# A graph layer's edge sums: a quarter of the late chunk products as two float32r parts, a larger share of the sort comparisons on VectorE, and the folding of weights in sixteen steps

## The chip, the cores and the metric

The kernel runs on one NeuronCore of a Trainium2 chip. The metric is the device time of one execution in microseconds (us). The engines are TensorE (PE, with its weight loads shown as PEld), VectorE (DVE), ScalarE (ACT), GpSimd (POOL) and SyncE (SP, which here only issues DMAs). Each engine runs its instructions in program order.

## What is computed

A message-passing layer of a graph network. 206,250 edges carry a row of 128 float32 values each; the rows are summed by the node named in `src`; the sums go through three dense layers together with the node rows `x` and a global row; the result is added to `x` and normalised.

```
edge_aggr = zeros((n, 128)).at[row].add(edge_features)        # n = 6250 nodes
combined  = concat([x, edge_aggr, global_expand], -1) @ W_c + b_c
h = softplus(combined @ W1 + b1)
h = softplus(h @ W2 + b2)
out = layernorm(x + (h @ W3 + b3))
```

## The kernel before

The nodes are cut into 32 buckets of 196 (`BL`). The edges lie in 1692 columns of 122 rows; two columns make a pair, so there are 846 pairs, in eight groups; three pairs make a piece (`PAIRS`), which gives 286 pieces. The work has three stages, most of it overlapped:

- **Sort and scatter.** For each group the positions of its edges are worked out (`positions`: counting matmuls in bf16 and small DVE steps, lines 498 to 764; line 498 compares `pair_block` with a table, both in SBUF). For each piece a one-hot matrix of 6 x 128 columns is made from the edges' slots (`compare`, lines 1137 to 1142): on DVE as one comparison with a table in PSUM, on ACT as six `Abs` activations and one `Relu`. Even pieces are DVE's, odd ones ACT's (`SHARE = 2`). `gather` (line 1153) sorts the rows by a matmul with this matrix, two units of three matmuls a piece; `settle` (line 1165) copies each unit from PSUM into one of six pair buffers (`SETS`), two ACT copies a unit; `scatter_row` (line 1182) writes one pair's rows to their places in `rows_by` in HBM by an indirect DMA that POOL issues: 846 of them. Places that may stay empty are filled beforehand (`fill_rows`, DMAs on SP from a constant tile of 7 rows a partition, `FILL`).
- **Sum.** `rows_by` comes back in chunks of 128 rows, each with rows of one bucket only (or of two neighbours). `load` brings up to eight chunks into one of six buffers (`AHEAD`), by SP; `match` (line 990) makes a one-hot matrix of 196 columns a chunk on DVE, with the table of nodes in PSUM; `product` (line 1013) multiplies, one float32 matmul a chunk, which the trace shows as two records (1758 products, 3516 records); `add` (line 1036) adds the finished PSUM sums into `sums_t`, on DVE. The unit of match and product is up to four chunks (`HALF`); there are 512 units.
- **Layers.** `node_layers` (lines 1356 to 1440) runs the dense layers tile by tile, with `Abs`, `Exp` and `Ln` on ACT and the maxima, sums and statistics on DVE. `fold` and the biases (`c_bias`, `z_bias`, `b2_c`, `b3_all`) are folded from the weights by `node_rows`, ahead of that.

The order is written out by a planner in the kernel. Every step gets a planned time: a scattered row every 1.3 us (`SCATTER`) from 24 us (`FIRST`), comparisons, gathers and evictions so many us ahead of their rows (`COMPARED`, `GATHERED`, `SETTLED`), the steps of an ACT comparison spread over 0.65 us each, from `SPREAD` earlier on; each load after its rows are scattered, each match two units ahead of its product (`TOGETHER`; four in the tail, `AT_END`), each product when the one before it is planned to be over. The steps sorted by time are the program of PE, DVE, ACT and SP. What is planned later than the last row (1123.8 us) is the rest, which `node_layers` takes up between its tiles, in the same order. The two steps of `node_rows` (lines 1070 to 1097) are planned in the second half of the fourth group.

Of the kernel before, what the change touches and what calls it, by code (L numbers as in the profile page):

```python
# [6 lines left out]

F32 = mybir.dt.float32
BF16 = mybir.dt.bfloat16
F16 = mybir.dt.float16  # L10
# [8 lines left out]
P = 128  # L19

BL = 196
# [29 lines left out]

FILL, DUE = 7, 8
ROW = 136
# [93 lines left out]
def kernel(  # L147
# [171 lines left out]
    with ExitStack() as phase:  # L319
        rows_p = phase.enter_context(tc.tile_pool(name="rows", bufs=ROWS))  # L320
        sort_p = phase.enter_context(tc.tile_pool(name="sort", bufs=3))
        pairs_in = phase.enter_context(tc.tile_pool(name="pairs_in", bufs=2))
# [28 lines left out]
        def scratch(name):  # L351
            return per.tile([P, 4 * P], F32, name=name, bufs=1)

# [52 lines left out]
        def fill_rows():  # L406
# [10 lines left out]
            def some(due, b, n, lo, rows, k):  # L417
                to = rows_by.rearrange("(s j) c -> s j c", j=STRIDE * P)[b:b + n, lo:lo + rows * k, :]
                ins = sync_dma(to.rearrange("b (p k) c -> p b (k c)", k=k),
                               fill[:rows, :k * ROW].unsqueeze(1).to_broadcast([rows, n, k * ROW]))  # L420
                apart(ins, "direct", ["scatter"])
                fills.setdefault(due, []).append(ins)

            def doubtful(b, mixed):
                if mixed:
                    start, end, twice, room, per = ROOM * P, STRIDE * P, 2, MIXED_ROOM / 2, MIXED_PER
                else:
                    start, end, twice, room, per = 0, rooms[b] * P, 1, rooms[b], ROWS_PER[kind[b]]
                lo = start + twice * int(certain(mixed, gap_at, room, per))
                hi = end - twice * untouched(mixed, per)  # L430
                rows, k = min(((rows, -(-(hi - lo) // rows)) for rows in (96, 112, P)),
                              key=lambda e: (e[0] * e[1], -e[0]))
                assert k <= FILL and lo + rows * k <= end
                return lo, rows, k
# [451 lines left out]
        def sum_steps():  # L886
# [36 lines left out]
            base_of = {v: min(bs) for v, bs in in_visit.items()}  # L923
            chunks, hots_of, parts_of, met, begun = {}, {}, {}, {}, set()
            awaits = [0]
# [52 lines left out]

            def match(n):
                j, a, e = units_of[n]  # L980
                hot = hots.tile([P, HALF, BL], F32, name="hot")
                hots_of[n] = hot
                q = a
                while q < e:
                    lo = hi = place_in(j, q)
                    step, m = 1, 1
                    while q + m < e and place_in(j, q + m) > hi and (m == 1 or place_in(j, q + m) == hi + step):
                        step, hi = place_in(j, q + m) - hi, place_in(j, q + m)
                        m += 1
                    nc.vector.tensor_tensor(  # L990
                        hot[:, q - a:q - a + m],
                        chunks[j][:, lo:hi + 1:step, D:W].to_broadcast([P, m, BL]),
                        iota_ps.unsqueeze(1).to_broadcast([P, m, BL]), op=ALU.is_equal)
                    q += m

            pending = []

            def product(n):
# [9 lines left out]
                for q in range(a, e):  # L1008
# [3 lines left out]
                    last = met[v].count(b) == in_visit[v].count(b)  # L1012
                    nc.tensor.matmul(part[:, b - base_of[v], :], t[:, place_in(j, q), :D], hot[:, q - a],  # L1013
                                     start=first, stop=last)
                if n == last_unit[j]:
# [24 lines left out]
            found, load_at, match_at, product_at, freed, at = [], {}, [], {}, {}, 0.0  # L1040
            opened = -1
            for n, (j, a, e) in enumerate(units_of):
# [23 lines left out]
        def node_rows():  # L1066

            steps = []

            def combine():  # L1070


                small = small_bank()
                nc.tensor.matmul(small[:, 0, :1], of_weights["wc2"], cols[:, 3:4],
                                 start=True, stop=True)
                nc.vector.tensor_add(c_bias, small[:, 0, :1], cols[:, 0:1])
                small = small_bank()
                for k in range(2):
                    nc.tensor.matmul(small[:, k, :], of_weights[f"wc{k}"], w_sb["w1"],
                                     start=True, stop=True)  # L1080
                nc.vector.tensor_copy(fold, small[:, :2, :])

            def biases():
                small = small_bank()
                nc.tensor.matmul(small[:, 0, :1], w_sb["w1"], c_bias, start=True, stop=True)
                nc.vector.tensor_add(z_bias, small[:, 0, :1], cols[:, 1:2])

                nc.vector.tensor_scalar(neg_z, z_bias, -1.0, None, op0=ALU.mult)
                small = small_bank()
                nc.tensor.matmul(small[:, 0, :1], w_sb["w2"], z_bias, start=True, stop=True)  # L1090
                nc.vector.tensor_add(b2_c, small[:, 0, :1], cols[:, 2:3])
                nc.vector.tensor_scalar(neg_b2, b2_c, -1.0, None, op0=ALU.mult)
                b2_all = per.tile([P, P], F32, name="b2_all", bufs=1)
                nc.vector.tensor_scalar(b2_all, ones, b2_c, None, op0=ALU.mult)
                small = small_bank()
                nc.tensor.matmul(small[:, 0, :], b2_all, w_sb["w3"], start=True, stop=True)
                nc.vector.tensor_add(b3_all, small[:, 0, :], of_weights["b3"])

            return [combine, biases]

# [30 lines left out]
        def compare(i):  # L1131
# [3 lines left out]
            hot = hot_of[i] = sort_p.tile([P, 2 * PAIRS, P], F32, name="sort_hot")  # L1135
            if i % SHARE == 0:
                return [lambda: nc.vector.tensor_tensor(  # L1137
# [56 lines left out]
        with tc.manual_schedule(engines={ET.PE, ET.DVE, ET.Activation, ET.SP}):  # L1194
# [71 lines left out]
            for i, t in enumerate(begins):  # L1266
                mine = units(i)
                soon = 0.0 if i else SOON
                if i % SHARE == 0:
                    when(t - COMPARED - soon, lambda i=i: compare_next(i))  # L1270
# [346 lines left out]
```

## Time and profile before

| | |
|---|---|
| median of 3 runs | 1289.03 us (1283.15 to 1290.0) |
| the profiled execution | 1289.92 us |
| its span in the trace | 1288.2 us |
| PE busy | 1167.7 us (91%) |
| DVE busy | 1027.6 us (80%) |
| ACT busy | 1003.9 us (78%) |
| POOL busy | 880.9 us (68%) |
| DMA, mean | 297 GB/s, 381.96 MB |

A row of waits reads: engine and line, what it waited for, us in total, times, longest. A row of groups reads: line, engine, operation, tiles, shapes, count, then the busy time in us and the mean ns of one, then the idle time ahead of them and what ended it. A row of the sums by stretch gives the stretch and its length, the busy time and count of each engine, the granted TensorE clock, the DMA engines' share and GB/s. A row of the timeline or of the chain of waits begins with start and duration in us.

### The profile page before, as it was taken

What the parts mean: (1) busy time and instruction counts of PE and PEld (TensorE: products, weight loads), DVE (VectorE), ACT (ScalarE), POOL (GpSimd) and SP (SyncE); (2) the same over time, 40 slices, a digit from 0 to 9 for tenths busy, and PEclk for the clock granted to TensorE, in tenths of its full rate; (3) what the DMA queues carried; (4) which work ended last, traced back from release to release, by engine and by line L of the source; (5) the groups of instructions that cost most, each with busy time, mean ns of one, the idle gap of its engine ahead of it and who ended that gap; (6) DMA issues with size and microseconds to landing.
All of it is one profiled execution on the core that took longest, in us unless ns stands there. A gap on an engine that the chain in (4) does not pass through costs nothing.

```text
span 1288.2 us, 26304 instructions
## 1 busy us (share of the span) xinstructions
PE 1167.7 (91%) x8617; PEld 1111.8 (86%) x8617; DVE 1027.6 (80%) x2260; ACT 1003.9 (78%) x2335; POOL 880.9 (68%) x915
## 2 busy tenths in 40 slices
PE   5778898888998998999899999999999999899893
PEld 5667788877988898989899999999999999898772
DVE  7868977888789977899878887789876767687784
ACT  5897987899687888977998888988899999403343
POOL 2777777777577776776777777777777777750334
PEclk9788998989999998999999999999999999999996
DMA  6789998899999997997999999999999999874421
GB/s 248 240 296 347 344 334 288 305 344 355 339 327 331 362 330 278 319 325 246 322 309 309 323 336 328 345 313 335 316 350 334 369 336 363 288 218 140 140 75 53
DMA packets 174636, 381.96 MB, mean 297 GB/s; under 512 B 27546, under 2 KB 118626, under 8 KB 160670
## 3 DMA queue, kind: packets, MB, share of 16 engines
q1 hardware_dynamic: 130751, 260.70, 61.2%
q0 software_dynamic: 41328, 115.65, 23.1%
q10 hardware_dynamic: 2415, 3.85, 0.9%
q8 instruction: 72, 1.18, 0.4%
q14 instruction: 70, 0.57, 0.1%
HBM read 242.47 MB, written 142.20 MB: 299 GB/s over the span
## 4 chain that ended last, share of the span: by engine, by line
PE 65%; DVE 12%; ACT 8%; DMA 7%; issue 4%; POOL 3%; SPq 0%; ACTq 0%; DVEq 0%; POOLq 0%
PE part L1013 37%; PE sorted L1153 21%; ACT pairs L1165 4%; DMA rows_by<-pairs,pair 4%; POOL rows_by L1182 3%; ACT sort_hot L1140 3%; DMA chunks<-rows_by 3%; DVE hot L990 2%; DVE past L727 1%; PE small L557 1%; PE small L559 1%; ACT sort_hot L1142 1%; DVE sort_hot L1137 1%; DVE sums_t L1036 1%; PE small L1395 1%
## 5 line engine op out<-in xcount | busy, mean ns | idle before, releaser
L1182 POOL DMA_INDIRECT rows_by<-pairs,pair x846 | 828.1, 979 | 298.3 <-issue 202.8
L1013 PE MATMUL part<-hot,chunks 128*128 128x196 f32 x3516 | 675.1, 335 | 13.2 <-DVE sums_t L1036 9.9
L1165 ACT COPY pairs<-sorted 64x387 f32<-64x387 f32 (+2 forms) x1144 | 542.6, 474 | 118.8 <-PE sorted L1153 95.7
L1013 PEld LDWEIGHTS part<-hot,chunks 128*128 128x128 f32 x3516 | 582.0, 193 | 21.9 <-DVE sums_t L1036 11.3
L1153 PE MATMUL sorted<-rows,sort_hot 122*128 122x129 f32 x3384 | 498.5, 288 | 44.5 <-ACT sort_hot L1142 32.0
L1153 PEld LDWEIGHTS sorted<-rows,sort_hot 122*128 122x128 f32 x3384 | 457.6, 199 | 53.5 <-ACT sort_hot L1142 36.3
L990 DVE TENSOR_TENSOR hot<-chunks,both_ps 128x784 f32<-128x784 f32 (+3 forms) x541 | 426.1, 809 | 9.2 <-DMA chunks<-rows_by 9.0
L1140 ACT ACTIVATE sort_hot<-plain,slot 122x128 f32<-122x128 f32 x840 | 292.8, 394 | 18.6 <-PE sorted L1153 6.3
L1036 DVE TENSOR_TENSOR sums_t<-sums_t,part 128x392 f32<-128x392 f32 (+1 forms) x262 | 143.5, 548 | 134.0 <-PE part L1013 133.0
L1137 DVE TENSOR_TENSOR sort_hot<-slot,both_ps 122x768 f32<-122x768 f32 x143 | 134.5, 940 | 1.9 <-PE sorted L1153 1.0
L1142 ACT ACTIVATE sort_hot<-sort_hot 122x768 f32<-122x768 f32 x143 | 118.6, 830 | 3.9
L1437 POOL TENSOR_SCALAR y<-y,mv,rs 128x128 f32<-128x128 f32 x40 | 31.1, 785 | 93.8 <-DVE rs L1425 93.5
L576 DVE TENSOR_REDUCE slot<-small 122x16 f32<-122x512 f32 (+2 forms) x109 | 72.9, 668 | 21.5 <-PE small L559 20.7
L1367 ACT ACTIVATE away<-sorted,z_bias 128x512 f32<-128x512 f32 (+2 forms) x13 | 8.5, 656 | 72.9 <-PE sorted L1357 72.9
L498 DVE TENSOR_TENSOR pair_ib<-pair_block,plain 122x512 bf16<-122x512 bf16 (+2 forms) x157 | 63.4, 411 | 0.2
L557 PE MATMUL small<-pair_ib,half 122*122 122x512 bf16 (+2 forms) x109 | 43.3, 398 | 7.6 <-DVE slot L576 7.5
L742 PEld LDWEIGHTS <-past 128*128 128x128 f16 x424 | 25.4, 100 | 17.9 <-DVE past L727 12.7
L727 DVE TENSOR_TENSOR past<-both_ps,starts 128x512 f16<-128x512 f32 (+1 forms) x61 | 39.8, 664 | 1.2 <-PE small L742 0.9
L742 PE MATMUL small<-jump,past 128*128 128x56 f16 (+3 forms) x424 | 29.4, 190 | 11.8 <-DVE past L727 8.4
L559 PEld LDWEIGHTS <-starts_h 128*122 128x122 bf16 x236 | 25.3, 148 | 11.9 <-issue 7.7
L1114 ACT COPY rows<-pair_i 122x16 f32<-122x16 f32 x106 | 22.2, 209 | 17.0 <-DMA rows<-in_edge 16.4
L727 DVE TENSOR_TENSOR past<-both_ps,starts_late 128x512 f16<-128x512 f32 (+2 forms) x49 | 32.3, 661 | 0.0
(163 smaller groups left out, 515.6 us busy)
## 6 DMA issues: line engine op xcount, KB each, us to landing
rows<-in_edge SPq DMA_DIRECT2D x105, 1032.0 KB
chunks<-rows_by SPq DMA_DIRECT2D x362, 136.0 KB
chunks<-rows_by SPq DMA_DIRECT2D x203, 204.0 KB
chunks<-rows_by SPq DMA_DIRECT2D x75, 272.0 KB
rows_by<-pairs,pair POOLq DMA_INDIRECT x846
rows_by<-fill SPq DMA_DIRECT2D x10, 1249.5 KB
rows_by<-fill SPq DMA_DIRECT2D x10, 714.0 KB
chunks<-rows_by SPq DMA_DIRECT2D x13, 408.0 KB
```

Source lines behind the costliest of these rows:

```text
L498: nc.vector.tensor_tensor(ib, cols.unsqueeze(2).to_broadcast([PN, m, SB, QUAD]), bucket_at[:PN].unsqueeze(1).to_broadcast([PN, m, SB, QUAD ...
L576: nc.vector.tensor_reduce(to, of, axis=mybir.AxisListType.X, op=ALU.max)
L727: nc.vector.tensor_tensor(past[:, :, a:b], twice_ps[:KB].unsqueeze(1).unsqueeze(1).to_broadcast([KB, 2, b - a, P // 2]), own["starts"][:, ...
L990: nc.vector.tensor_tensor(hot[:, q - a:q - a + m], chunks[j][:, lo:hi + 1:step, D:W].to_broadcast([P, m, BL]), iota_ps.unsqueeze(1).to_bro ...
L1013: nc.tensor.matmul(part[:, b - base_of[v], :], t[:, place_in(j, q), :D], hot[:, q - a], start=first, stop=last)
L1036: nc.vector.tensor_add(here, here, of)
L1137: return [lambda: nc.vector.tensor_tensor(hot[:PN, :2 * m], slot[:PN, at:at + 2 * m].unsqueeze(2).to_broadcast([PN, 2 * m, P]), slot_ps[:P ...
L1140: return [lambda j=j: nc.scalar.activation(hot[:PN, j], by_slot[:PN], AF.Abs, bias=slot[:PN, at + j:at + j + 1], scale=-1.0) for j in rang ...
L1142: for j in range(2 * m)] + [lambda: nc.scalar.activation(hot[:PN, :2 * m], hot[:PN, :2 * m], AF.Relu, bias=1.0, scale=-1.0)]
L1153: nc.tensor.matmul(out[:, j, :], hot[:PN, at], rows_at[col // LOAD_COLS][:PN, col % LOAD_COLS, :], start=True, stop=True)
L1165: nc.scalar.copy(sets_at[i][64 * n:64 * n + 64, lo:lo + m, h, :W], out[64 * h:64 * h + 64, :m, :])
L1182: s = nc.gpsimd.indirect_dma_start(out=dst, out_offset=bass.IndirectOffsetOnAxis(ap=at, axis=0), in_=rows[:, j].rearrange("p a b -> p (a b ...
```

## The change

Five things change together.

- **Fine units.** Of the units planned later than 650 us, every fourth (every third after the last row is planned) is multiplied in two float32r parts, if it has over two chunks that lie in one run; units planned from 30 us before to 12 us after the last row are left out. ACT copies the unit's rows to a float32r tile (`high`), DVE writes the rest, rows minus high, over the rows (`low`), and each chunk takes two float32r matmuls, high and rest, instead of one float32 matmul.
- **Sort comparisons.** Of five pieces two are ACT's (the second and the fourth) and three DVE's; ACT's steps are planned 4.5 us ahead instead of 2; there are four buffers for the one-hot matrices instead of three.
- **Folding.** `node_rows` is sixteen steps (three of them empty) instead of two, spread over the same time.
- **Fill.** The constant tile has 4 rows a partition instead of 7, and a fill of more is issued as two DMAs.
- **Buffers.** Five instead of six `hot` tiles, `scratch` tiles of half the width, two `high` tiles.

```diff
-FILL, DUE = 7, 8
+FILL, DUE = 4, 8
-SHARE, SPREAD = 2, 2.0
+BY_ACT, SHARE, SPREAD = (1, 3), 5, 4.5
+FINE_FROM, FINE_EVERY, HIGHS, COARSE = 650.0, (4, 3), 2, (-30.0, 12.0)
-    hots = ctx.enter_context(tc.tile_pool(name="hots", bufs=6))
+    hots = ctx.enter_context(tc.tile_pool(name="hots", bufs=5))
-        sort_p = phase.enter_context(tc.tile_pool(name="sort", bufs=3))
+        sort_p = phase.enter_context(tc.tile_pool(name="sort", bufs=4))
-                ins = sync_dma(to.rearrange("b (p k) c -> p b (k c)", k=k),
-                               fill[:rows, :k * ROW].unsqueeze(1).to_broadcast([rows, n, k * ROW]))
+                to = to.rearrange("b (p k) c -> p b (k c)", k=k)
+                for a in range(0, k, FILL):
+                    w = min(FILL, k - a) * ROW
+                    ins = sync_dma(to[:, :, a * ROW:a * ROW + w],
+                                   fill[:rows, :w].unsqueeze(1).to_broadcast([rows, n, w]))
...
+            def high(n):
+                high_of[n] = sums_p.tile([P, HALF, D], F32R, name="high", bufs=HIGHS)
+                for to, at, m in runs_of(n):
+                    nc.scalar.copy(high_of[n][:, to], chunks[units_of[n][0]][:, at, :D])
+
+            def low(n):
+                for to, at, m in runs_of(n):
+                    rows = chunks[units_of[n][0]][:, at, :D]
+                    nc.vector.tensor_tensor(rows.bitcast(F32R), rows, high_of[n][:, to].bitcast(F32),
+                                            op=ALU.subtract)
...
-                    nc.tensor.matmul(part[:, b - base_of[v], :], t[:, place_in(j, q), :D], hot[:, q - a],
-                                     start=first, stop=last)
+                    rows, by = t[:, place_in(j, q), :D], hot[:, q - a]
+                    if n in fine:
+                        nc.tensor.matmul(part[:, b - base_of[v], :], high_of[n][:, q - a], by,
+                                         start=first, stop=False)
+                        nc.tensor.matmul(part[:, b - base_of[v], :], rows.bitcast(F32R), by,
+                                         start=False, stop=last)
+                    else:
+                        nc.tensor.matmul(part[:, b - base_of[v], :], rows, by.bitcast(F32),
+                                         start=first, stop=last)
...
+                since += 1
+                if (product_at[n] > FINE_FROM and since >= FINE_EVERY[product_at[n] > ends[-1]]
+                        and not COARSE[0] < product_at[n] - ends[-1] < COARSE[1] and e - a > 2 and len(runs_of(n)) == 1):
+                    since = 0
+                    fine.add(n)
+                    found.append((max(match_at[n], product_at[n] - 4.0), len(found), lambda n=n: high(n)))
+                    found.append((max(match_at[n] + 1.0, product_at[n] - 1.5), len(found), lambda n=n: low(n)))
...
-            return [combine, biases]
+            return [
+                lambda: product_of("c", (of_weights["wc2"], cols[:, 3:4], 1)),
+                lambda: product_of("fold", *((of_weights[f"wc{k}"], w_sb["w1"], D) for k in range(2))),
+                lambda: v.tensor_add(c_bias, got("c"), cols[:, 0:1]),
+                lambda: v.tensor_copy(fold, banks_of["fold"][:, :2, :]),
+                lambda: product_of("z", (w_sb["w1"], c_bias, 1)),
+                lambda: None,
...
-            if i % SHARE == 0:
+            if i % SHARE not in BY_ACT:
```

More of the change, by code (lines that the diff above doesn't have):

```diff
@@ L1066, in node_rows @@
         def node_rows():
[L1068 to L1097, printed above, removed]
@@ L1099, in node_rows, with product_of, got, b2_rows @@
-            return [combine, biases]
+            banks_of, v = {}, nc.vector
+            def product_of(name, *pairs):
+                small = banks_of[name] = small_bank()
+                for k, (of, by, w) in enumerate(pairs):
+                    nc.tensor.matmul(small[:, k, :w], of, by, start=True, stop=True)
+            def got(name, k=0, w=1):
+                return banks_of[name][:, k, :w]
+            b2_all = []
+            def b2_rows():
+                b2_all.append(per.tile([P, P], F32, name="b2_all", bufs=1))
+                v.tensor_scalar(b2_all[0], ones, b2_c, None, op0=ALU.mult)
```

45 lines of the change are left out of this document (31 added, 14 removed).

## The prediction

> **What bounds the kernel now.** I read the 40 slices first, then the waits, then sums by stretch, the groups by shape, and the timeline where a price was missing.
>
> ```profile
> POOL 2777777777577776776777777777777777750334
> ```
> ```profile
> core 0: us, PE busy (x) PEld busy (x) DVE busy (x) ACT busy (x) POOL busy (x), PEclk, DMA share, GB/s
> 60.00:650.00 590.00, 523.17 (x4154) 500.38 (x4155) 491.31 (x1173) 499.10 (x1173) 434.81 (x444) 0.95 0.91 321
> 650.00:1110.00 460.00, 458.80 (x3393) 453.82 (x3392) 357.56 (x598) 410.82 (x965) 350.48 (x360) 1.00 0.96 330
> 1128.00:1157.00 29.00, 29.00 (x163) 28.79 (x164) 24.50 (x40) 0.00 (x0) 15.47 (x16) 0.94 0.73 211
> 1157.00:1260.00 103.00, 95.75 (x485) 76.98 (x484) 80.57 (x194) 42.62 (x71) 22.17 (x30) 1.00 0.39 117
> ```
>
> Three stages, each with its own limit. The scatter stage issues 846 rows on GpSimd (POOL). Its waits, first for 60 to 650 us, then for 650 to 1110 us:
>
> ```profile
> POOL rows_by L1182 <- issue: 108.9, 355, 0.6
> POOL rows_by L1182 <- DMA rows_by<-pairs,pair: 19.9, 35, 6.4
> POOL rows_by L1182 <- ACT pairs L1165: 16.9, 28, 2.1
> POOL rows_by L1182 <- ACT sort_hot L1140: 4.5, 11, 1.5
> POOL rows_by L1182 <- ACT rows L1114: 1.2, 2, 0.9
> ```
> ```profile
> POOL rows_by L1182 <- issue: 83.3, 273, 0.3
> ```
>
> The idle time before a row is never under about 0.30 us (83.3 / 273 = 0.305, the longest 0.3), and the row itself takes 0.97 to 0.98, so a row costs 1.277 us whatever feeds it. From 650 us on, every wait is that floor: POOL runs at its own rate. Before 650 us there are real holes, which are each total less 0.30 a time: 19.9 - 10.5 = 9.4 us put down to DMA, and 16.9 - 8.4 = 8.5, 4.5 - 3.3 = 1.2 and 1.2 - 0.6 = 0.6 us put down to ScalarE (ACT), 19.7 us in all. Only these can be won in the scatter stage.
>
> TensorE's (PE) waits, 60 to 650 us and then 650 to 1110 us:
>
> ```profile
> PE sorted L1153 <- ACT sort_hot L1142: 29.9, 21, 2.2
> PE sorted L1153 <- ACT pairs L1165: 8.4, 10, 3.6
> PE small L742 <- DVE past L727: 7.9, 11, 1.8
> ```
> ```profile
> PE small L557 <- DVE slot L576: 0.8, 1, 0.8
> PE sorted L1153 <- ACT pairs L1165: 0.3, 1, 0.3
> ```
>
> Early on PE waits above all for ACT's sort comparisons. From 650 to 1110 us it waits 1.1 us of 460: it is full too, just keeping pace with POOL. After the last row (1128 us) comes the tail, PE-bound to about 1260 us with VectorE (DVE) close behind, then a short chain of last layers.
>
> **The change part by part.** Durations:
>
> ```profile
> L1165 ACT COPY pairs<-sorted 64x387 f32<-64x387 f32 x1116 | 534.4, 479 | 116.8 <-PE sorted L1153 94.1 <-DMA rows_by<-pairs,pair 3.3 <-PE part L1013 2.6
> L1140 ACT ACTIVATE sort_hot<-plain,slot 122x128 f32<-122x128 f32 x840 | 292.8, 394 | 18.6 <-PE sorted L1153 6.3 <-DVE slot L576 5.8
> L990 DVE TENSOR_TENSOR hot<-chunks,both_ps 128x784 f32<-128x784 f32 x230 | 218.2, 963 | 7.7 <-DMA chunks<-rows_by 7.6
> L990 DVE TENSOR_TENSOR hot<-chunks,both_ps 128x588 f32<-128x588 f32 x223 | 166.0, 759 | 1.5 <-DMA chunks<-rows_by 1.4
> L1137 DVE TENSOR_TENSOR sort_hot<-slot,both_ps 122x768 f32<-122x768 f32 x141 | 133.4, 946 | 1.5 <-ACT pairs L1165 0.7 <-PE sorted L1153 0.6
> L1142 ACT ACTIVATE sort_hot<-sort_hot 122x768 f32<-122x768 f32 x138 | 116.3, 843 | 3.9
> L1368 ACT ACTIVATE away<-away 128x512 f32<-128x512 f32 x22 | 13.9, 630 | 0.7
> L359 DVE TENSOR_TENSOR first<-first,second 122x248 f32<-122x248 f32 x4 | 1.7, 417 | 0.1
> ```
>
> *Sort comparisons.* There are 286 pieces. ACT's share falls from 143 to 114, DVE's rises from 143 to 172. On ACT a piece is 6 x 0.394 + 0.843 = 3.21 us, on DVE 0.946. At POOL's full rate a piece has 3 x 1.277 = 3.83 us; ACT needs 4 x 0.479 of evictions and on average 1.60 of comparisons, 3.52 us (92%), afterwards 1.92 + 0.4 x 3.21 = 3.20 (84%). Its comparisons also start 2.5 us earlier in the plan (SPREAD) with a fourth buffer. So the 29.9 us that PE waits for them should mostly go, and with them the holes put down to ACT: 8.5 + 1.2 = 9.7 us (the 0.6 waits for an edge load). I take -9.7; the ends are 0 and all 19.7. What is late next is DVE: some 15 more pieces before 650 us, 14 us on top of 491 of 590 (83% becomes 86%). PE's waits for DVE there (7.9 the largest) may grow, but DVE stays under ACT's old load.
>
> *Fine units.* Evaluating the planner's formulas with the new constants gives 76 fine units: 55 with 185 products between 650 and 1094 us of the plan (20 of four products, 35 of three), 21 with 81 products in the tail. Each adds one ACT copy (0.63 us for 512 columns), one DVE subtraction and two float32r matmuls per product instead of one f32 product, which the trace shows as two records.
>
> ```profile
> 1011.46 2.32 PE part L1013 x14
> 1013.79 1.34 PE sorted L1153 x12
> ```
> ```profile
> 885.89 0.39 PE L559 MATMUL small<-half,starts_h_late 128*122 128x128 bf16 x4
> 886.11 0.89 PE L1153 MATMUL sorted<-rows,sort_hot 122*128 122x129 f32 x6
> ```
>
> An f32 record of 196 columns costs 2.32 / 14 = 166 ns, a product 0.333 us. No float32r appears. From below: four bf16 matmuls of 128 columns start 0.22 us ahead of the next, 55 ns each, so one pass over 196 columns is 84 ns. From above: each is like a whole f32 product, 333. Between: f32 weights are seen to load at a pace of 1.34 / 12 = 112 ns. Each matmul loads f32-wide weights, so I take 112, the row nearest in kind: 0.224 a product, 0.109 saved. (The Trainium skill, page "FP8 and Floating Point Precision", section "TensorE Precision Notes", says true FP32 makes four passes and a reduced-precision mode truncates the 4-byte value; two passes for four would save 167 ns, 81 x 0.167 = 13.5 us in the tail. No trace here shows float32r.)
>
> Before 1094 us, 185 x 0.109 = 20 us of PE time is freed where POOL sets the pace, so I cost it at nothing: what hides it is POOL's 1.277 us per row. It is reserve, which PE needs if the earlier holes close. ACT gets about 30 us of copies and loses 12 pieces x 3.21 = 39: level. DVE gets about 33 + 11 on 358 of 460: under 90%.
>
> *The subtraction beside the scatter.* By the slope of the 588 and 784 rows (1.04 ns a column) it takes 0.68 us for 512 columns, 0.55 for 384; the 417 ns for 248 columns lies on about the same line. Unlike match and the comparisons, whose second operand is in PSUM, it has both inputs in SBUF, as the counting line 498 has (pair_block and a table):
>
> ```profile
> 857.09 0.97 POOL L1182 DMA_INDIRECT rows_by<-pairs,pair  x1 [0.31 <-issue]
> 858.25 0.42 DVE L498 TENSOR_TENSOR pair_ib<-pair_block,plain 122x512 bf16<-122x512 bf16 x1
> 858.37 1.14 POOL L1182 DMA_INDIRECT rows_by<-pairs,pair  x1 [0.30 <-DMA rows_by<-pairs,pair]
> ```
>
> The op still runs 0.30 us into a row that started after it, and the row takes 0.17 us longer than its neighbour; the first 0.13 us costs nothing. For an op at a random phase of 1.277 us the mean delay is (0.68 - 0.13)^2 / 2 / 1.277 = 0.118 us, and 0.069 for the shorter one: 20 x 0.118 + 35 x 0.069 = 4.8 us, straight onto POOL's path. I take +4.8, between 0 and 33 (each op stopping a row for its whole length). The Trainium skill, "SBUF — State Buffer", section "SBUF: two separate sides", speaks against this part of the change: whichever of DVE (two SBUF inputs against a GpSimd op that reads SBUF) and GpSimd starts first holds the shared ports for its whole instruction; the row above agrees in kind but shows 0.17 us for an op of 0.42.
>
> *Tail.* It runs 264 products. The chain of waits has the run of them before the first layer:
>
> ```profile
> 1127.95 28.81 PE part L1013 x162
> ```
>
> With some 15 before it these 81 products are the first 96, and hold 7 fine units (25 products): PE saves 2.7 us in the stretch to 1157 us, but DVE gets 4 x 0.68 + 3 x 0.55 = 4.4 on 24.5 of 29: it fills up, so I count 0. The other 14 units (56 products) save PE 6.1 us of the 103 to 1260 us, and DVE gets 9.5 on 80.6. I take -5; the ends are -13.4 (84 ns a record: 81 x 0.165) and +3.
>
> *Folding in sixteen steps.* The two blocks hold DVE up once for long:
>
> ```profile
> DVE z_bias L1086 <- PE small L1085: 4.5, 1, 4.5
> ```
>
> It goes, but it lies around 470 us, where DVE's lateness reaches POOL only as a hole, and the holes are counted above; alone it would be at most those 4.5 us.
>
> *Fill, buffers.* A fill over four rows a partition is issued as two DMAs:
>
> ```profile
> rows_by<-fill SPq DMA_DIRECT2D x10, 1249.5 KB
> ```
>
> The bytes are the same; ten of these and the two of 408 KB split, 12 more issues on SP over 400 us, ahead of loads queued behind them. I take 0 (+-2: finer packets might end a late fill earlier or later). One hot buffer fewer leaves five for a lead of four: nothing.
>
> Sum: -9.7 + 4.8 - 5 = -9.9. The profiled execution took 1289.92 us (span 1288.2), so 1280.0; the median of the runs shown, 1289.03, lies 0.9 lower: **1279 us**.
>
> **The rivals.** (Times as for the median; a measurement of this kernel can tell about 0.5%, 6.4 us, from no change.)
> - *Everything is won.* All 19.7 us of holes close, DVE costs 2, the tail saves 11: 1289 - 28.7 = 1260. For it: PE's long waits for ACT. Against: half of the holes wait for DMA, with its engines 91% busy.
> - *Transfers keep the holes.* 4 us of holes go, the tail saves 2, the subtraction gives 4.8 back: 1288, no change. For it: the 9.4 us put down to DMA.
> - *DVE becomes the bound.* PE waits for DVE's extra comparisons instead of ACT's: the holes stay and grow by 5 (a third of the 14 us), plus 4.8, plus 3 in the tail (80.6 + 9.5 + the 15.5 below = 105.6 of 103): 1302, slower. It decides from the point where DVE's idle time in a stage is less than what is added.
> ```profile
> DVE y L1403 <- PE small L1395: 15.5, 9, 2.6
> ```
>  Against: most of that idle time is waiting for PE, which gets faster.
> - *The whole lock.* Each subtraction before 1094 us stops a row for all its length, 33 us: 1289 - 9.7 + 33 - 5 = 1307. Against: line 498's 0.17 of 0.42.
> - *float32r is no cheaper at 196 columns.* Each matmul costs a whole f32 product: 266 x 0.333 = 89 us on a PE that waits 1.1 of 460 us: 1289 - 9.7 + 4.8 + 89 = 1373. Nothing in the trace excludes it.
>
> **How the numbers follow.** Forecast 0.56 (own range 1268 to 1284), everything won 0.12, transfers 0.15, DVE 0.08, whole lock 0.04, float32r 0.05. Faster by over 0.5% (below 1282.6): 0.12 and nearly all of 0.56, 0.65. Within: 0.15 and the forecast's upper edge, 0.18. Slower: 0.17. The range 1260 to 1297 leaves out the last two, half of DVE's case and the edge of the first.
>
> **What would show it.** Right: before 650 us PE's wait for ACT's comparisons falls from 29.9 to under 10 us; POOL's holes before 650 us fall to about 10; rows after 650 us stay at 1.277 but for some 20 longer ones beside the subtraction; last row near 1123 us; float32r records near 112 ns; last row to end about 155 us instead of 160. Wrong: float32r records above 166 ns; PE waiting for DVE in the scatter stage by tens of us; holes moved to DMA.

## The result, and the profile after

The changed kernel is slower: 1305.63 us median (1303.43 to 1309.19, 5 runs) against 1285.76 us (1283.15 to 1290.0, 5 runs, among them the three of the table ahead of the prediction) for the kernel before on the same chip. The ratio is 1.0145, with a 95% interval of 1.0119 to 1.0172. The profiled execution took 1309.19 us, its span is 1307.3 us.

The page of the changed kernel, in its 40 slices, shows one slice that looks unlike its neighbours: the 35th, 1111 to 1144 us.

```profile
POOL 2777777777677777777777777777777777800334
PEclk9888999998999999999999999999999999799996
```

The TensorE clock drops to 0.7 there and GpSimd is busier than in any other slice. The sums by stretch of the changed kernel, cut at that place, say more:

```profile
core 0: us, PE busy (x) PEld busy (x) DVE busy (x) ACT busy (x) POOL busy (x), PEclk, DMA share, GB/s
60.00:650.00 590.00, 522.79 (x4215) 497.39 (x4215) 509.67 (x1203) 460.76 (x1098) 443.88 (x452) 0.97 0.93 326
650.00:1110.00 460.00, 443.62 (x3346) 431.19 (x3346) 390.21 (x654) 386.34 (x912) 351.12 (x355) 1.00 0.95 325
1126.00:1142.00 16.00, 1.82 (x11) 1.59 (x10) 15.18 (x4) 0.98 (x2) 15.42 (x15) 0.61 0.39 120
1142.00:1165.00 23.00, 19.91 (x110) 18.87 (x110) 18.66 (x32) 3.39 (x6) 0.00 (x0) 0.87 0.45 128
```

Up to 1110 us things went as forecast: ACT fell from 499 to 461 us before 650 us, PE from 459 to 444 us after it. Then there are 16 us in which PE does 1.8 us of work and DVE is "busy" for 15.2 us with four instructions. The timeline of the changed kernel names them (start, duration):

```profile
1124.52 0.98 POOL L1220 DMA_INDIRECT rows_by<-pairs,pair  x1 [0.30 <-issue]
...
1125.59 15.82 POOL L1494 TENSOR_TENSOR x_sb<-x_sb,b_all 128x512 f32<-128x512 f32 x15
...
1126.82 0.97 DVE L1002 TENSOR_TENSOR hot<-chunks,both_ps 128x784 fp32r<-128x784 f32 x1 [1.08 <-DMA chunks<-rows_by]
1127.71 13.40 DVE L1015 TENSOR_TENSOR chunks<-chunks,high 128x512 fp32r<-128x512 f32 x1
...
1141.16 0.53 PE L1039 MATMUL part<-hot,chunks 128*128 128x196 f32 x1 [14.18 <-DVE chunks L1015]
...
1142.77 4.41 PE L1042 MATMUL part<-hot,chunks 128*128 128x196 f32 x14
...
1142.80 0.51 ACT L1010 CAST high<-chunks 128x384 fp32r<-128x384 f32 x1 [15.39 <-PE part L1037]
...
1146.84 0.69 DVE L1015 TENSOR_TENSOR chunks<-chunks,high 128x512 fp32r<-128x512 f32 x1
...
1147.77 0.27 PE L1037 MATMUL part<-hot,high 128*128 128x196 f32 x1
1147.88 0.28 PE L1039 MATMUL part<-hot,chunks 128*128 128x196 f32 x1
1147.99 0.27 PE L1037 MATMUL part<-hot,high 128*128 128x196 f32 x1
```

After the last row GpSimd adds `b3` to the node rows, 15 additions back to back (line 1494 here, 1456 before), all operands in SBUF. The first subtraction of the tail has both inputs in SBUF too. It takes 13.40 us; the next one of the same shape takes 0.69. PE waits 14.18 us for it, ACT's next copy stands behind PE for 15.39, and when PE goes on its clock is down: 14 float32 records take 4.41 us, where before they took 2.32. In the kernel before, the same 15 additions ran at the same place, and DVE's work beside them, whose second operand is in PSUM, kept its usual length. Two rows of the timeline of before:

```profile
1128.12 15.46 POOL L1456 TENSOR_TENSOR x_sb<-x_sb,b_all 128x512 f32<-128x512 f32 x15
```
```profile
1130.76 0.97 DVE L990 TENSOR_TENSOR hot<-chunks,both_ps 128x784 f32<-128x784 f32 x1 [1.01 <-DMA chunks<-rows_by]
```

The waits of the changed kernel answer the other steps. POOL's, 60 to 650 us, and then PE's, 60 to 650 us and from 1110 us on:

```profile
POOL rows_by L1220 <- DMA rows_by<-pairs,pair: 18.1, 46, 1.9
POOL rows_by L1220 <- ACT pairs L1203: 12.6, 33, 1.2
```
```profile
PE sorted L1191 <- ACT pairs L1203: 22.1, 34, 2.0
PE sorted L1191 <- DVE sort_hot L1175: 9.9, 4, 4.8
```
```profile
PE part L1039 <- DVE chunks L1015: 23.7, 9, 14.2
PE part L1042 <- DVE sums_t L1065: 4.6, 2, 3.2
```

PE's 29.9 us of waiting for ACT's comparisons is gone from the list; waits for the evictions (22.1) and for DVE's comparisons (9.9) stand in its place. POOL's holes, which are the idle time ahead of the rows beyond 0.305 us each, summed over all gaps longer than 0.4 us, fell from 20.1 to 9.7 us.

### The profile page after: what moved, and what is told of

It is laid out like the page before. It is cut to its first block, busy times and chain, and to the rows that moved or that the text cites. A ratio compares the mean times of both kernels' runs of the same rounds, so it can differ in the third digit from the quotient of the medians.

```text
span 1307.3 us, 26451 instructions
## 1 busy us (share of the span) xinstructions
PE 1147.5 (88%) x8617; PEld 1079.3 (83%) x8617; DVE 1100.8 (84%) x2365; ACT 952.0 (73%) x2226; POOL 889.5 (68%) x915
## 4 chain that ended last, share of the span: by engine, by line
PE 44%; DVE 21%; DMA 13%; issue 7%; POOL 7%; ACT 6%; SPq 1%; ACTq 0%; DVEq 0%; POOLq 0%
PE part L1042 22%; PE sorted L1191 14%; DMA rows_by<-pairs,pair 7%; POOL rows_by L1220 7%; DMA chunks<-rows_by 5%; DVE hot L1002 5%; ACT pairs L1203 3%; DVE sort_hot L1175 2%; DVE past L732 2%; DVE chunks L1015 2%; PE part L1039 2%; ACT sort_hot L1178 2%; DVE sums_t L1065 1%; PE part L1037 1%; DVE pair_ib L503 1%
## 5 line engine op out<-in xcount | busy, mean ns | idle before, releaser
L1042 PE MATMUL part<-hot,chunks 128*128 128x196 f32 x2984 | 579.0, 336 | 12.3 <-DVE sums_t L1065 7.0
L1042 PEld LDWEIGHTS part<-hot,chunks 128*128 128x128 f32 x2984 | 495.4, 193 | 17.7 <-DVE sums_t L1065 7.8
L1002 DVE TENSOR_TENSOR hot<-chunks,both_ps 128x784 f32<-128x784 f32 (+5 forms) x541 | 428.3, 810 | 11.2 <-DMA chunks<-rows_by 6.8
L1178 ACT ACTIVATE sort_hot<-plain,slot 122x128 f32<-122x128 f32 x684 | 228.9, 392 | 8.6 <-DVE slot L581 5.8
L1175 DVE TENSOR_TENSOR sort_hot<-slot,both_ps 122x768 f32<-122x768 f32 (+2 forms) x172 | 159.6, 928 | 5.3 <-PE sorted L1191 5.1
L1475 POOL TENSOR_SCALAR y<-y,mv,rs 128x128 f32<-128x128 f32 x40 | 32.3, 814 | 114.0 <-DVE rs L1463 113.7
L1180 ACT ACTIVATE sort_hot<-sort_hot 122x768 f32<-122x768 f32 x114 | 95.9, 841 | 0.2
L1010 ACT CAST high<-chunks 128x512 fp32r<-128x512 f32 (+1 forms) x76 | 42.3, 559 | 73.0 <-PE part L1037 30.3
L1039 PE MATMUL part<-hot,chunks 128*128 128x196 f32 x266 | 68.1, 291 | 28.6 <-DVE chunks L1015 28.2
L1039 PEld LDWEIGHTS part<-hot,chunks 128*128 128x128 f32 x266 | 52.6, 198 | 34.7 <-DVE chunks L1015 32.6
L1037 PE MATMUL part<-hot,high 128*128 128x196 f32 x266 | 74.1, 308 | 3.0 <-DVE sums_t L1065 3.0
L1015 DVE TENSOR_TENSOR chunks<-chunks,high 128x512 fp32r<-128x512 f32 (+1 forms) x76 | 59.8, 787 | 16.3 <-ACT high L1010 16.3
L1037 PEld LDWEIGHTS part<-hot,high 128*128 128x128 f32 x266 | 52.3, 197 | 5.3 <-issue 5.2
```

The costliest lines, as they stand in the source:

```text
L1002: nc.vector.tensor_tensor((hot if n in fine else hot.bitcast(F32))[:, to], chunks[j][:, at, D:W].to_broadcast([P, m, BL]), iota_ps.unsquee ...
L1015: nc.vector.tensor_tensor(rows.bitcast(F32R), rows, high_of[n][:, to].bitcast(F32), op=ALU.subtract)
L1037: nc.tensor.matmul(part[:, b - base_of[v], :], high_of[n][:, q - a], by, start=first, stop=False)
L1039: nc.tensor.matmul(part[:, b - base_of[v], :], rows.bitcast(F32R), by, start=False, stop=last)
L1042: nc.tensor.matmul(part[:, b - base_of[v], :], rows, by.bitcast(F32), start=first, stop=last)
L1175: return [lambda: nc.vector.tensor_tensor(hot[:PN, :2 * m], slot[:PN, at:at + 2 * m].unsqueeze(2).to_broadcast([PN, 2 * m, P]), slot_ps[:P ...
```

## The experiments

Three figures are read from every trace: when the last row ends, how long the tail is from there to the span's end, and by how much the rows after 650 us are longer than 0.972 us. Since a run that reaches its last row later has fewer products left at that point, a fourth one is fairer to the tail: the time from the start of the last 243 products (486 records in every kernel) to the end. Five executions with ordinary products in the tail (before, e1, e2, e6, e7) have 156.7 to 158.1 us there. (In e5 what is lost lies just ahead of these products, in the changed kernel within them.)

| run | ratio to before, 95% | last row | tail | last 243 products | longer rows after 650 us |
|---|---|---|---|---|---|
| before | | 1128.0 | 160.1 | 157.8 | 1.2 |
| after | 1.0145 (1.0119 to 1.0172) | 1125.5 | 181.8 | 181.6 | 7.0 |
| e1_no_fine | 0.996 (0.9946 to 0.9974) | 1120.4 | 159.9 | 156.8 | 1.6 |
| e2_no_tail_fine | 0.9989 (0.9977 to 1.0001) | 1121.7 | 156.2 | 156.7 | 7.0 |
| e3_tail_fine_later | 0.9991 (0.9978 to 1.0005) | 1124.4 | 162.0 | 161.1 | 7.6 |
| e4_no_x_add | 1.0008 (0.9984 to 1.0031) | 1122.6 | 164.0 | 162.9 | 6.3 |
| e5_sbuf_table | 1.0086 (1.0059 to 1.0113) | 1125.3 | 176.9 | 157.1 | 1.6 |
| e6_share_only | 0.9956 (0.994 to 0.9973) | 1120.4 | 159.5 | 157.9 | 1.2 |
| e7_fold_and_fill | 0.9966 (0.9949 to 0.9982) | 1122.4 | 162.1 | 158.1 | 2.4 |
| e8_tail_only | 0.9972 (0.9949 to 0.9995) | 1119.5 | 161.5 | 158.3 | 1.7 |
| e9_tail_no_low | 0.9953 (0.9932 to 0.9974) | 1116.6 | 159.1 | 155.4 | 1.4 |
| e10_no_low_no_match | 0.9899 (0.9859 to 0.9939) | 1116.7 | 156.7 | 152.9 | 2.0 |
| e11_no_match | 0.9923 (0.9898 to 0.9947) | 1121.4 | 154.2 | 153.9 | 1.5 |

The traces let the fourth figure be split. From the last product's end to the end of the span it is 29.8 to 30.3 us in every run. What lies before that is PE's idle time, what a lowered clock costs, and the rest, PE's work at full clock. The cost of the clock is worked out: in some stretches, 3.41 us long or a multiple of that, the traces give a granted clock of 0.5, and half of PE's busy time in them is counted as lost.

| last 243 products, us | PE's work | PE idle | lowered clock |
|---|---|---|---|
| before, e1, e2, e5, e6, e7 | 119.4 | 7.1 | 0 to 1.4 |
| after | 112.3 | 29.5 | 9.5 |
| e3_tail_fine_later | 113.7 | 12.4 | 4.7 |
| e4_no_x_add | 112.4 | 16.2 | 4.5 |
| e8_tail_only | 113.9 | 12.4 | 1.7 |
| e9_tail_no_low | 113.8 | 10.3 | 1.1 |
| e10_no_low_no_match | 113.4 | 7.5 | 1.7 |
| e11_no_match | 118.9 | 4.8 | 0 |

The six traces with ordinary products there agree in work and in idle time within 0.03 us each, so that the 1.4 us between them are the clock.

"Two-part units" are the fine units of the change. My theory was that the long subtraction against GpSimd's run of additions makes the loss (the port theory of the expectations below). The rivals were the two-part products as such, with their copies, their subtractions and records that cost more than 112 ns (the chain theory), and the other parts of the change (the third theory).

**e1_no_fine**: no two-part units at all.

```diff
-FINE_FROM, FINE_EVERY, HIGHS, COARSE = 650.0, (4, 3), 2, (-30.0, 12.0)
+FINE_FROM, FINE_EVERY, HIGHS, COARSE = 1.0e9, (4, 3), 2, (-30.0, 12.0)
```

> The changed kernel without any fine unit; the new share of comparisons, the folding in sixteen steps, the split fills and the buffers stay. Port theory (a VectorE subtraction with both inputs in SBUF and GpSimd's work on SBUF shut each other out: 5.9 us on the scattered rows after 650 us, and 13.4 us for one subtraction behind GpSimd's additions at the head of the tail): the last row ends near 1119 us instead of 1125.5, the tail is the old 160 us, 1281 us in all, faster than before (1286). Chain theory (the fine units of the tail cost by themselves, since each product waits for a copy and a subtraction on busy engines): the same 1281. Third theory (the other parts of the change cost the time): 1295 or more.

It takes 1280.83 us against 1286.18: faster than both kernels. The two-part units make all of the loss, and the other parts together are worth 0.4%.

**e2_no_tail_fine**: two-part units up to the last row only.

```diff
-FINE_FROM, FINE_EVERY, HIGHS, COARSE = 650.0, (4, 3), 2, (-30.0, 12.0)
+FINE_FROM, FINE_EVERY, HIGHS, COARSE = 650.0, (4, 10 ** 9), 2, (-30.0, 12.0)
```

> The changed kernel with the 55 fine units of the scatter stage and none in the tail. Port and chain theory: last row near 1125.5 us, tail 160 us, 1287 us in all, and some 6 us more than without any fine unit, from rows that are longer beside a subtraction. Third theory: 1300.

1283.43 us; the tail is that of ordinary products, so the 20 us are lost in the tail. The rows after 650 us are longer by 7.0 us in all, as in the changed kernel, against 1.6 in e1: that is the price of the subtractions beside the scatter. Of these 5.4 us the medians of the two runs show 2.6 (1283.43 against 1280.83).

**e3_tail_fine_later**: in the tail, two-part units only from 55 us after the planned last row, past the additions.

```diff
-FINE_FROM, FINE_EVERY, HIGHS, COARSE = 650.0, (4, 3), 2, (-30.0, 12.0)
+FINE_FROM, FINE_EVERY, HIGHS, COARSE = 650.0, (4, 3), 2, (-30.0, 55.0)
```

> The changed kernel with the fine units of the tail beginning 55 us after the last planned row instead of 12, when GpSimd's additions of the bias to x are over. Port theory: no subtraction over 0.8 us, no TensorE wait of 14 us, tail 181.8 - 12.7 for the long subtraction - some 3 for the cold clock behind it = 166 us or less, 1290 us in all. Chain theory: the tail stays over 175 us, 1300 us in all.

1285.6 us, the tail 162.0 instead of 181.8, as the port theory had it. The last 243 products still take 161.1 us: PE's work is 5.7 us less than with ordinary products, but PE stands 5.3 us more, and the clock costs 4.7.

**e4_no_x_add**: the changed kernel without GpSimd's additions.

```diff
                 x_of[n0] = node_rows_of(ahead, n0, w, len(tiles), load=nc.scalar.dma_start)
-                for lo, hi, r in blocks_of(w):
-                    nc.gpsimd.tensor_tensor(
-                        x_of[n0][:r, lo:hi, :], x_of[n0][:r, lo:hi, :],
-                        b3_all[:r].unsqueeze(1).to_broadcast([r, hi - lo, D]), op=ALU.add)
```

> The changed kernel without GpSimd's fifteen additions of b3 to the node rows (the output lacks b3); all 76 fine units as they are. Port theory: the first subtraction of the tail falls from 13.4 to 0.7 us, tail near 166 us, 1290 us in all. Chain theory: the subtraction's 13.4 us had another cause, the tail stays over 175 us, 1302 us.

1287.88 us, the tail 164.0. The same subtraction, at the same place, in this run's timeline:

```profile
1124.67 0.97 DVE L1002 TENSOR_TENSOR hot<-chunks,both_ps 128x784 fp32r<-128x784 f32 x1 [1.40 <-DMA chunks<-rows_by]
1125.56 0.68 DVE L1015 TENSOR_TENSOR chunks<-chunks,high 128x512 fp32r<-128x512 f32 x1
```

With the subtraction kept and the additions gone, it takes 0.68 us. So it is the two together.

**e5_sbuf_table**: the kernel before, with ordinary products only, but three matches at the head of the tail compare with a table in SBUF instead of PSUM. If two SBUF inputs against the additions are the cause, a match must be struck as well.

```diff
-    hots = ctx.enter_context(tc.tile_pool(name="hots", bufs=6))
+    hots = ctx.enter_context(tc.tile_pool(name="hots", bufs=5))
...
-                        iota_ps.unsqueeze(1).to_broadcast([P, m, BL]), op=ALU.is_equal)
+                        (iota_sb if n in by_sbuf else iota_ps).unsqueeze(1).to_broadcast([P, m, BL]),
+                        op=ALU.is_equal)
...
+                if product_at[n] > ends[-1] + 12.0 and len(by_sbuf) < 3:
+                    by_sbuf.add(n)
```

> The kernel before, with no fine unit at all; only the matches of three units at the head of the tail read their table of 196 nodes from SBUF instead of PSUM (and five hot buffers for six, to make room). Port theory: the first of the three that runs into GpSimd's additions to x lasts until they are over, 10 to 13 us instead of 0.96, TensorE waits for it, and the time is 12 to 18 us longer, about 1300 us. Rival (the long subtraction was a matter of float32r, of writing in place or of waiting for ScalarE's copy): all three last 0.76 to 0.96 us, no change, 1286 us.

1301.99 us against 1288.25; the forecast of the port theory, about 1300, is met. Its timeline:

```profile
1124.29 0.97 POOL L1186 DMA_INDIRECT rows_by<-pairs,pair  x1 [0.30 <-issue]
...
1124.99 16.14 DVE L991 TENSOR_TENSOR hot<-chunks,iota_sb 128x784 f32<-128x784 f32 x1 [2.02 <-DMA chunks<-rows_by]
...
1125.37 16.08 POOL L1461 TENSOR_TENSOR x_sb<-x_sb,b_all 128x512 f32<-128x512 f32 x15
...
1141.53 0.96 DVE L991 TENSOR_TENSOR hot<-chunks,iota_sb 128x784 f32<-128x784 f32 x1
```

The first of the three matches takes 16.14 us instead of 0.96, in a kernel without a float32r instruction; the second, behind the run, takes its usual time. The place of the operand is the cause, not the kind of product.

**e6_share_only and e7_fold_and_fill**: e1 taken apart. e6 is e1 with the old folding and a fill of 7 rows; e7 is e1 with the old share of the comparisons.

```diff
-FILL, DUE = 4, 8
+FILL, DUE = 7, 8
...
-            return [
-                lambda: product_of("c", (of_weights["wc2"], cols[:, 3:4], 1)),
...
+            return [combine, biases]
```
```diff
-BY_ACT, SHARE, SPREAD = (1, 3), 5, 4.5
+BY_ACT, SHARE, SPREAD = (1,), 2, 2.0
...
-        sort_p = phase.enter_context(tc.tile_pool(name="sort", bufs=4))
+        sort_p = phase.enter_context(tc.tile_pool(name="sort", bufs=3))
```

> The changed kernel without fine units, with the two folding steps and the unsplit fills of before: what is left is the new share of comparisons, their earlier start and the buffers. Share theory (the comparisons closed the holes that GpSimd had before 650 us): 1281 us, as without any fine unit. Rival (the split fills and the folding closed them, above all the hole of 6 us behind a fill): 1286 us.

> The changed kernel without fine units and with every second piece's comparisons on ScalarE, planned 2 us ahead, in three buffers, as before: what is left is the folding in sixteen steps, the split fills and the buffers. Share theory: 1286 us. Rival (fills and folding): 1281 us.

1283.26 and 1284.87 us against 1288.25: each part alone is faster than before, by 0.4 and 0.3%, and the intervals of e1, e6 and e7 overlap. PE's waits of 60 to 650 us, first e6, then e7:

```profile
PE sorted L1189 <- ACT pairs L1201: 19.5, 29, 2.0
PE sorted L1189 <- DVE sort_hot L1173: 10.4, 4, 4.9
```
```profile
PE sorted L1191 <- ACT sort_hot L1180: 28.1, 19, 2.2
PE sorted L1191 <- ACT pairs L1203: 10.2, 11, 3.6
```

The share alone takes PE's wait for ACT's comparisons away, as the prediction had it; the folding and fill leave it at 28.1. Yet POOL's holes are 12.0 us in e6 and 10.0 in e7, against 20.1 in before and 10.3 in e1. The two don't add up. The holes also differ between executions: e5, which has the sort, the fill and the folding of before, has 15.8, and none of its holes is longer than 2.3 us, where before has one of 6.05. Nine traces have both parts (the changed kernel, e1 to e4 and e8 to e11); their holes are 6.1 to 10.3 us. So either part alone brings the holes most of the way down; how much of it is each part's own stays open.

**e8_tail_only**: two-part units only from 55 us after the planned last row, none before.

```diff
-FINE_FROM, FINE_EVERY, HIGHS, COARSE = 650.0, (4, 3), 2, (-30.0, 12.0)
+FINE_FROM, FINE_EVERY, HIGHS, COARSE = 1150.0, (4, 3), 2, (-30.0, 55.0)
```

> The changed kernel with fine units in the tail alone, from 55 us after the last planned row on (14 units). By the prediction's own count, TensorE's saving of 6 us lies on the path: 1276 us, 5 us faster than without fine units (1281). Chain theory, now for what is left of the tail's loss: VectorE's subtraction takes the saving back, 1281 to 1284 us.

1284.23 us, the tail 161.5. Away from the additions and from the rows the two-part units still gain nothing: 112 records at 0.113 us instead of 0.166 save PE 112 x 0.053 = 5.9 us, but the last 243 products take 158.3, 0.2 above the longest of the ordinary ones. PE's work falls by 5.5 us, its idle time grows by 5.3, and the clock costs 1.7.

**e9_tail_no_low**: e8 without the subtraction.

```diff
-                        nc.tensor.matmul(part[:, b - base_of[v], :], rows.bitcast(F32R), by,
+                        nc.tensor.matmul(part[:, b - base_of[v], :], high_of[n][:, q - a], by,
                                          start=False, stop=last)
...
-                    found.append((max(match_at[n] + 1.0, product_at[n] - 1.5), len(found), lambda n=n: low(n)))
```

> This is the kernel with two-part units in the tail alone, without the step that makes the low part: the second float32r matmul of a chunk takes the high part again, so the output lacks the low parts of 14 units, and TensorE has the same matmuls. Theory (the two-part units save TensorE some 6 us in the tail, and the wait for the subtractions takes it back): the tail from the last row's end falls from 161.5 us to 154 to 157, and the time to 1276 to 1280 us. Rival (the saving isn't on the path, TensorE waits for something else in these units): the tail stays at 159.5 to 162 and the time at 1281 to 1285.

The tail is 159.1 us. My theory (154 to 157) missed; the rival's lower edge is 0.4 us above. PE's waits of 1110 us to the end, first e8, then e9:

```profile
PE part L1039 <- DVE chunks L1015: 6.2, 3, 2.5
PE part L1042 <- DVE sums_t L1065: 4.7, 2, 2.9
...
PE part L1037 <- DVE sums_t L1065: 3.0, 2, 1.9
PE sorted L1395 <- DVE sums_t L1065: 2.2, 2, 1.6
```
```profile
PE sorted L1394 <- DVE sums_t L1065: 4.8, 5, 1.6
PE part L1042 <- DVE sums_t L1065: 4.2, 2, 3.9
PE part L1037 <- DVE sums_t L1065: 4.1, 3, 1.7
```

With the 6.2 us for the subtraction gone, the waits for DVE's additions into the sums grow from 9.9 to 13.1. By the last 243 products the gain is 2.9 us over e8: 2.1 of PE's idle time, 0.6 of the clock and 0.1 of its work.

**e10_no_low_no_match and e11_no_match**: DVE is relieved in 14 units of the tail, with two-part products (e10) and with ordinary ones (e11). The same edit is in both; e11's products are float32 and have no copy.

```diff
+                if n in fine and kept:
+                    hots_of[n] = kept[0]
+                    return
...
-                    rows, by = t[:, place_in(j, q), :D], hot[:, q - a]
+                    rows, by = t[:, place_in(j, q), :D], hot[:, 0 if n in fine else q - a]
```

> Without the low step the tail was 159.1 us, hardly shorter than the 159.9 without any two-part units. This kernel is that one with VectorE relieved as well: of the 14 two-part units of the tail only the first makes its one-hot matrix, of one chunk, and all products of these units use it, so the output is not the reference's sums. That takes some 12 us of matches from VectorE. New theory (the tail has two limits close together, TensorE and VectorE: relieving TensorE alone turns into waits for VectorE, relieving both shortens the tail): the tail falls to 151 to 156 us and the time to 1273 to 1279 us. Rival (TensorE's waits in the tail come from the written order, not from VectorE's load): the tail stays at 158 to 160.

> VectorE alone relieved: these 14 units leave out the matches as in the run beside it (the output is not the reference's sums), but their products are ordinary float32 matmuls and ScalarE makes no copies. New theory (two limits close together): TensorE is the limit again, the tail stays at 158 to 161 us, and the time at 1278 to 1283 us. Rival (VectorE alone is the limit of the tail): the tail falls to 151 to 156 here already. Rival (the written order): 158 to 160 in both.

The tails are 156.7 and 154.2 us: neither is where my theory of two limits had it, and e11 fell to where the rival "VectorE alone" had it. But e11 reached its last row with 243.5 products left, e10 with 248, 1.5 us of work, and the clock differs by 1.7. The split above is clearer. With PE alone relieved (e9) its work falls by 5.6 us and its idle time grows by 3.2; with both relieved (e10) its work falls by 6.0 and the idle time grows by only 0.4; with DVE alone relieved of 13.4 us of matches (e11) the work falls by 0.5 and the idle time by 2.3. So VectorE's load decides how long TensorE stands. That relieving PE alone turns into waits for DVE, and relieving both doesn't, is what the theory of two limits said; its forecast for e11 missed that the ordinary tail has waits for DVE too. Most of what DVE was spared came to nothing. Its waits in e11, 1115 to 1245 us (in e1 these three are 14.1, 4.3 and 1.3):

```profile
DVE y L1445 <- PE small L1437: 18.4, 9, 3.1
DVE hot L1013 <- DMA chunks<-rows_by: 7.2, 6, 2.8
DVE sums_t L1070 <- PE part L1047: 6.4, 7, 1.3
```

Which steps of the written order cost how much of this was not taken further.

## Why the prediction was wrong, step by step

- **Tail: this step failed.** It said -5, between -13.4 and +3; it was +21.7 (160.1 to 181.8). It priced every subtraction of the tail at 0.68 or 0.55 us by its shape, and weighed the ports that DVE and GpSimd share only against scattered rows. GpSimd's run of additions stood in a row that it quoted, 15.47 us of POOL busy in 1128 to 1157 us, and was not read as an instruction with SBUF operands. The additions make 17.8 us of the difference (181.8 against 164.0 in e4): 12.7 are the subtraction's extra length, and the lowered clock from there on costs 5.0 us more than in e4 (9.5 against 4.5). The step's other half failed too: even without that collision the tail was 4.1 us longer than e1's (164.0 against 159.9), and in e8 1.7, where 5 us less were forecast. What went wrong there is not PE's saving: the changed kernel's 81 two-part products cut its work by 7.1 us (119.4 to 112.3), where 2.7 + 6.1 were counted. The step set only DVE's load against that saving and put PE's waits and the clock at nothing. In e4 PE stands 9.1 us more than with ordinary products, and waits 10.0 us for subtractions; the clock costs 4.5 us, against about 1 in before.
- **float32r: right.** The records start 0.11 us apart (1147.77, 1147.88, 1147.99), against the 112 ns taken from the sort's weight loads. The figure worked out from the Trainium skill (page "FP8 and Floating Point Precision", section "TensorE Precision Notes"), 167 ns saved a product, isn't met: the records at this pace save 2 x (166 - 112) = 108 ns.
- **Subtraction beside the scatter: right.** Forecast +4.8; the rows after 650 us are longer by 7.0 instead of 1.2 us in all, +5.8. In the changed kernel 28 of them are over 0.985 us, and 23 of these run beside a subtraction. The row below, from its timeline, is one of the longest; the next one has the usual length. The rival of the whole lock, 33 us, is out.

```profile
1088.10 0.69 DVE L1015 TENSOR_TENSOR chunks<-chunks,high 128x512 fp32r<-128x512 f32 x1 [2.05 <-ACT high L1010]
1088.20 1.44 POOL L1220 DMA_INDIRECT rows_by<-pairs,pair  x1 [0.30 <-ACT high L1010]
1089.94 0.97 POOL L1220 DMA_INDIRECT rows_by<-pairs,pair  x1 [0.30 <-issue]
```

- **Sort comparisons: right in size, the credit open.** Forecast -9.7; the holes fell by 10.4 us. PE's wait for ACT's comparisons went as forecast, and that is the share's doing (e6). But e7 shows the holes at 10.0 without it, by parts that the prediction put at 0, and e6 with it at 12.0: that the sum of the holes came out within 1 us of the forecast is in part luck.
- **Folding and fill at 0: not borne out.** e7, with these alone beside one buffer fewer, is faster than before by 0.2 to 0.5%, 3.4 us by the medians.
- **Nothing gained on PE before 1094 us: right.** PE's busy time of 650 to 1110 us fell by 15.2 us, the last row came no earlier for it: e1, without it, has its last row 5.1 us before the changed kernel's.

The last row was forecast at 1123.1 us (1128.0 - 9.7 + 4.8) and ended at 1125.5; the tail was forecast at 155.1 and was 181.8. Those two, 2.4 and 26.7 us, are the whole miss of 29 us on the profiled execution. The prediction's rivals that ended slower (DVE as the bound, the whole lock) gave about the measured time, but by mechanisms that the trace doesn't show.

## What to carry to other kernels

Before a DVE operation with two SBUF inputs is added, list everything that GpSimd does in that stretch, not only its main loop: a run of back-to-back GpSimd additions of two SBUF operands held such an operation until only the last addition was left, and with it all that waited for it. It is the kind of GpSimd work that counts: beside scattered rows and beside GpSimd's TENSOR_SCALAR runs the same subtraction kept its length (next section). One operand in PSUM, or a place past the run (e3), avoids the wait. And price what the relieved engine will wait for: here 5.5 to 6 us of TensorE's work came back as 5.3 us of waits where VectorE had to do more for it (e8), as 3.2 where VectorE did the same as before (e9), and as 0.4 where VectorE was relieved as well (e10). Short waits of TensorE cost clock as well (next section).

## What the runs showed of the hardware

- A DVE operation of 0.68 us took 13.40 us, and one of 0.96 took 16.14, beside 15 GpSimd additions back to back, eleven of 1.25 to 1.29 us and four short ones. The Trainium skill, page "SBUF — State Buffer", section "SBUF: two separate sides", says that whichever of the two starts first gets the shared ports for the whole instruction. That holds here in kind, but the wait was not for one instruction of 1.25 us: DVE got no turn between any two of the additions that ran while it waited, until only the last was left. In e5 the match was there 0.38 us ahead of the first addition, beside the last scattered row, and still waited. That DVE ran just ahead of the last addition is read from the ends (the operation ended 0.31 us before the run did in both) and from the length of the last addition, here in before, after and e5:

```profile
L1456 POOL TENSOR_TENSOR x_sb<-x_sb,b_all 114x128 f32<-114x128 f32 x1 | 0.4, 445 | 0.0
L1494 POOL TENSOR_TENSOR x_sb<-x_sb,b_all 114x128 f32<-114x128 f32 x1 | 0.9, 892 | 0.0
L1461 POOL TENSOR_TENSOR x_sb<-x_sb,b_all 114x128 f32<-114x128 f32 x1 | 1.2, 1177 | 0.0
```

- Not every GpSimd run does this. Later in the tail GpSimd runs TENSOR_SCALAR instructions on an SBUF tile back to back, 0.79 us each. In the changed kernel, e3, e4 and e8 together 15 subtractions fall beside them; each takes 0.68 to 0.74 us, and the GpSimd instruction that it delays takes 0.95 to 1.31. By the rule above the 12 that start while one is running would have waited for its end; they didn't. Beside scattered rows the 55 subtractions of the changed kernel took 0.55 to 0.69 us. Two rows from e8's timeline follow; one of the five instructions takes 1.10. Why GpSimd's additions and these differ is not shown.

```profile
1199.30 4.24 POOL L1475 TENSOR_SCALAR y<-y,mv,rs 128x128 f32<-128x128 f32 x5 [64.23 <-DVE rs L1463]
1201.41 0.68 DVE L1015 TENSOR_TENSOR chunks<-chunks,high 128x512 fp32r<-128x512 f32 x1
```

- The profile books this wait as the operation's own duration, not as idle time: DVE looks 95% busy (15.18 of 16 us) while it does next to nothing.
- In the other direction GpSimd lost little: the 15 additions took 15.82 us beside the subtraction and 15.46 without, and what they lost, the last one lost (0.45 us).
- PE stood for 14.18 us. The granted clock was 0.61 in that stretch (1126 to 1142 us) and 0.87 in the next (to 1165 us), and 14 float32 records took 4.41 us instead of 2.32.
- Short stands of PE cost clock too. While the last 243 products ran, the changed kernel's clock was at 0.5 for 17.07 us, from 2.6 us into the long stand on, and later four times for 3.41 us, which is 1.7 us lost each time. These four, and those of e3, e4, e8 and e10 after their first 10 us, all begin within 1.7 us of the end of a stand of 1.7 to 2.5 us. Not every such stand brings one: in e8 two of 2.52 us brought none. What decides is not shown.
